# Layer 0 of a four-layer network: blocks of the first and last image overlap, and the table is cleared in 163 small transfers

## The chip, the cores and the metric

The kernel runs on one core of one Trainium2 chip. A core has five engines that work side by side, each on its own list of instructions[...]: TensorE (PE) for matrix products, VectorE (DVE), ScalarE (ACT), GpSimd (POOL), and SyncE (SP), which here only issues transfers between the chip's memory (DRAM) and the on-chip buffer (SBUF). Sixteen DMA engines carry those transfers. PE writes its results to PSUM, a small memory of eight banks. An instruction that needs another engine's result waits on a semaphore, and everything behind it on its own engine waits too.

The metric is the device time of one execution in microseconds (us). Before the change it is 12985.0 us, the median of three runs from 12982.07 to 13003.0.

## The reference

Four images of 128 channels and 48 x 48 pixels go through four layers. The change touches layer 0 and the hand-over to layer 1. Layer 0, cut to what matters (`L` = 2304 pixels, `DI` = 256 inner channels, `K` = 4 scan directions, `N` = 16 states):

```python
def _L0_conv_ref(x, ...):
    def step(h, inp):
        u_t, d_t, B_t, C_t = inp
        dA = jnp.exp(d_t[..., None] * A)
        h = h * dA + (d_t * u_t)[..., None] * B_t[:, :, None, :]
        y = jnp.einsum('bkdn,bkn->bkd', h, C_t)
        return (h, y)
    ...
    xn = _layernorm(xi, ln1_g, ln1_b)
    xz = xn @ in_proj_w.T
    xc, z = jnp.split(xz, 2, axis=-1)
    xc = conv3x3_per_channel(xc) + conv_b          # cut
    xc = jax.nn.silu(xc)
    xs = jnp.stack([x_hw, x_wh, x_hw[..., ::-1], x_wh[..., ::-1]], axis=1)
    ...                                            # delta, B and C from xs
    out_y = _selective_scan(xs, delta, A, Bs, Cs, Ds)
    ...                                            # the four directions are added up to y
    y = _layernorm(y, outn_g, outn_b)
    y = y * jax.nn.silu(z)
    out = xi + y @ out_proj_w.T
```

Layer 1 is a deformable 3 x 3 convolution. Its first step is an ordinary 3 x 3 convolution of layer 0's output to 27 channels (18 offsets and 9 masks for each pixel); the pixels that the offsets point to are then gathered, with zeros outside the image:

```python
off_out = lax.conv_general_dilated(x, w_off, ..., padding='SAME') + b_off
o1, o2, mask = jnp.split(off_out, 3, axis=1)
...
sampled = _bilinear_gather(x, py, px) * mask[:, None]
```

Layers 2 and 3 are attention and mixture-of-experts layers on the same pixels; the change does not touch them.

## The kernel before

Layer 0 (`_layer0`) treats the four images one after another. For each image there are three kinds of work.

**Before the scans** (`pre`, written for one image). An image is cut into six blocks of 384 pixels. `before(im, j)` is a list of ten steps for one block: fetch `x` (L242), turn it on PE so that pixels lie on partitions (L247), copy it out of PSUM on ACT (L251), statistics on DVE with a power on POOL (L207 to L210), standardise on DVE (L214), turn back (L257), scale on ACT and store the result `xn` to DRAM for later (L261, L262), project to the two halves of the inner channels (L266), and copy each half into a padded image (L269). `merged(lists, lag)` joins the lists of the six blocks: list `i` starts `i * lag` steps late, and steps of the same time stand next to each other. With `lag` 10 the blocks simply follow one another. Then come 24 pieces of the per-channel 3 x 3 convolution (`convolve`: nine taps as 18 recorded matmuls, L187, and a copy with bias on ACT, L294) and `activate` (L302). `chained` joins lists so that the last step of one and the first step of the next share a place.

**The scans.** An image has 12 pieces (4 directions x 3 chunks of 768 pixels), each with 16 steps, one per state. A step is written out by hand in the loop at the end of `_layer0`: `row` loads one row of B to all partitions (L500, from the DRAM tensor `rows` that `prepare` stored at L372), `decay` (L505), `times_b` (L512 to L519), `scan` (L545), `turn` and `back` (L559, L573). Between the steps the loop calls `fill()` three times, which takes the next items from lanes: the preparation of the next piece, and an image lane that holds `post` of the image before and `pre` of the image after.

**After the scans** (`post`). `after(im, j)` has 18 steps for a block: fetch `y`, `xn` and `x` (L624 to L628), turn `y` (L634) and copy it (L641), statistics and standardising, turn back (L648), scale (L653), the gate's product (L663, L674), silu with two table loads on ACT (L677, L678), gating (L681), the output product (L686), the residual (L691), a copy into the padded image (L692), turn and store to `tok` (L697 to L702). When the last block is stored, four copies put `tok` into layer 1's `table` (L709). Then `offsets(im, j)`, nine steps for a block: 2 x 9 taps of the 27-channel convolution (L187), copy (L747), turn (L754), copy and store to `offs` (L760, L762).

For images 1 to 3 `pre`, and for images 0 to 2 `post`, lie in the lanes among the scans. `pre` of image 0 (the head) and `post` of image 3 (the tail) stand alone: `for s in pre(images[0]) + prepare(pieces[0], None)` ahead of the loop and `for s in post(images[-1])` behind it.

**PSUM and buffers.** The eight banks are shared out by pools: `ps` has two for the scans' turns, `pf` one, `pu` one for `prepare`, `yp` three and `b0` one. All steps of `before`, `convolve`, `after` and `offsets` take their PSUM from `psum()`, that is from the one bank of `pf`. SBUF buffers come from the pool `sp`, with two buffers for a name unless `bufs` says otherwise.

**The table.** Layer 1 gathers from `table`, which has a border of zeros around each image. It is cleared at the start (L169 to L173): the accumulator `y` is set to zero and written out ten times.

**Order.** The whole of layer 0 is under `manual_schedule` for PE, ACT, DVE and POOL, which keep the written order. SP is not among them: where a transfer stands in SP's list is decided by the planner of the framework, from its own idea of when things are ready.

Of the kernel before, what the change touches and what calls it, by code (L numbers as in the profile page):

```python
# [15 lines left out]
F32 = mybir.dt.float32  # L16
# [7 lines left out]
P = 128  # L24
# [15 lines left out]
CH = 768  # L40
# [59 lines left out]
]  # L100
NPI = len(PIECES)
TPC = CH // P
CT = 512
HBUF = 3
HB = BLK // 2
# [2 lines left out]
def _layer0(ctx, env, dr, io, table, offs):  # L108
# [16 lines left out]
    def load(name, shape):  # L125
        t = cp.tile(shape, F32, name=name)
        nc.sync.dma_start(t, io[name])
        return t

    def psum(*shape):  # L130
        return pf.tile(list(shape), F32, name="pf", tag="pf")

    ln_g = load("l0_ln_g", [P, 1])
# [27 lines left out]
    for pad in pads:  # L161
        nc.gpsimd.memset(pad, 0.0)


    u_hw = wp.tile([P, ND, L], F32, name="u_hw")
    u_wh = wp.tile([P, ND, L], F32, name="u_wh")
    y = wp.tile([P, ND, L], F32, name="y")
    zero = y.rearrange("p d f -> p (d f)")
    nc.gpsimd.memset(zero, 0.0)  # L169
    flat = table.rearrange("r c -> (r c)").rearrange("(p f) -> p f", p=P)  # L170
    for i in range(0, flat.shape[1], ND * L):
        w = min(ND * L, flat.shape[1] - i)
        nc.sync.dma_start(flat[:, i : i + w], zero[:, :w])  # L173


# [136 lines left out]

    def merged(lists, lag):

        out = []
        for t in range(max(i * lag + len(a) for i, a in enumerate(lists))):
            for i, a in enumerate(lists):
                if 0 <= t - i * lag < len(a):
                    out.append(a[t - i * lag])
        return out  # L320

    def chained(lists):
# [8 lines left out]
        return out  # L331

    def pre(im):
        items = merged([before(im, j) for j in range(NBLK)], 10)
        return items + chained([convolve(d, r) for r in range(L // HB) for d in range(ND)]) + [activate]

    class Piece:
# [279 lines left out]
    def after(im, j):  # L617

        cols = bass.ts(j, BLK)
        t = {}  # L620

        def fetch():
            t["yb"] = sp.tile([P, ND, BLK], F32, name="yb", bufs=1)
            nc.sync.dma_start(t["yb"], im.y[:, :, cols])  # L624
            t["xn"] = sp.tile([P, BLK], F32, name="xn")
            nc.sync.dma_start(t["xn"], im.xn[:, cols])
            t["xb"] = sp.tile([P, BLK], F32, name="xb")
            nc.sync.dma_start(t["xb"], io["x"][im.b][:, cols])  # L628

        def turn_y(g0, g1):  # L630
            t["pt"] = pt = psum(P, g1 - g0, DI)
            for g in range(g0, g1):
                for d in range(ND):
                    nc.tensor.transpose(  # L634
                        pt[:, g - g0, bass.ts(d, P)], t["yb"][:, d, bass.ts(g, P)], ident
                    )

        def turned(g0, g1):
            if g0 == 0:
                t["yt"] = sp.tile([P, G3, DI], F32, name="yt", bufs=1)  # L640
            nc.scalar.copy(t["yt"][:, g0:g1, :], t.pop("pt"))  # L641
            if g1 == G3:
                t["first"], t["second"] = standardise(t["yt"])

        def back_y(d):
            t["pt"] = pt = psum(P, BLK)
            for g in range(G3):
                nc.tensor.transpose(pt[:, bass.ts(g, P)], t["yt"][:, g, bass.ts(d, P)], ident)  # L648

        def normed(d):  # L650
            if d == 0:
                t["yn"] = sp.tile([P, ND, BLK], F32, name="yn", bufs=1)
            nc.scalar.activation(  # L653
                t["yn"][:, d, :],
                t.pop("pt"),
                AF.Identity,
                bias=ob[:, d : d + 1],
                scale=og[:, d : d + 1],
            )

        def gate(d):
            t["pz"] = psum(P, BLK)
            nc.tensor.matmul(  # L663
                t["pz"],
                ipT[:, DI + d * P : DI + (d + 1) * P],
                t["xn"],
                start=True,
                stop=True,
            )

        def gate_out(d):
            if d == 0:
                t["z"] = sp.tile([P, ND, BLK], F32, name="yt", bufs=1)
# [60 lines left out]

    def offsets(im, j):
        t = {}

        def third(i, n):
            if n == 0:
                t["pp"] = psum(NOFF, HB)  # L740
            taps(t["pp"], woT, pads[0], 2 * j + i, 3 * n, 3 * n + 3)

        def rows(i):
            if i == 0:
                t["fo"] = sp.tile([P, G3, DI], F32, name="yt", bufs=1)
                t["fo"] = t["fo"].rearrange("p g c -> p (g c)")[:NOFF, :BLK]
            nc.scalar.activation(  # L747
                t["fo"][:, bass.ts(i, HB)], t.pop("pp"), AF.Identity, bias=bo
            )

        def turn():
            t["pt"] = pt = psum(P, G3, NOFF)
# [22 lines left out]

    def post(im):
        return merged([after(im, j) for j in range(NBLK)], 18) + chained(
            [offsets(im, j) for j in range(NBLK)]
        )
# [21 lines left out]
                self.done += 1  # L801

    with tc.manual_schedule(engines=ORDERED):
        for s in pre(images[0]) + prepare(pieces[0], None):
            s()
        for g in range(3):
            do(row, g)
# [13 lines left out]
        for g in range(len(pieces) * NS + 2):  # L821
# [2 lines left out]
            if n == 0 and i + 1 < len(pieces):  # L824
                lanes["next"] = Lane(prepare(pieces[i + 1], pieces[i]), 3 * (NS - 3))
            if (p, n) == (0, 5) and b < NB:
                items = post(images[b - 1]) if b else []
                cols = [lambda d=d, j=j: columns(d, j) for j in range(NCH) for d in range(ND)]
                gap = len(items) // len(cols)
                for q, c in enumerate(cols):  # L830
# [33 lines left out]
            do(scan, g, 1)  # L864
        for d in range(ND):
            collect(pieces[-1], d)
        for s in post(images[-1]):
            s()

# [1359 lines left out]
```

## Time and profile before

| What | Value |
|---|---|
| Median of three runs | 12985.0 us (12982.07 to 13003.0) |
| Profiled execution | 12885.25 us |
| Its span, first to last instruction | 12883.3 us |
| Mean granted TensorE clock | 0.935 |
| Busy over the span | PE 87%, DVE 66%, ACT 54%, POOL 34% |
| First scan starts | 229.8 us |
| Last `y` accumulated | 5218.4 us |
| First and last gather of layer 1 | 5423.0 and 6332.9 us |

The profile is that of one execution, and all its times count from the start of its span. A row of the windows gives a stretch, its length, the busy time of each engine with the number of instructions, the mean TensorE clock that was granted (1.00 is full speed), the share of the 16 DMA engines' time in use, and GB/s. A row of the timeline gives start and length of one instruction or a run of equal ones, its line and shapes, and in brackets how long its engine had been idle and what ended that. A DMA row ends with the median time from a transfer's issue to its landing.

### The profile page before, as it was taken

How to read it: one execution, taken by the hardware profiler on the slowest of the kernel's cores; microseconds unless marked ns; L12 is line 12 of the kernel's file. 1: busy time of each engine (PE TensorE's matmuls, PEld its weight loads, DVE VectorE, ACT ScalarE, POOL GpSimd, SP SyncE). 2: the span in 40 equal slices, each digit the busy share in tenths (PEclk: the TensorE clock that was granted, in tenths of full speed). 3: DMA queues.
4: the chain of work that ended last, by engine and by line, in shares of the span. 5: the costliest groups of instructions: out<-in, count | busy, mean ns of one | idle time of the engine just before them, and what ended most of it. 6: DMA issues, size and time to landing. Idle time of an engine off the chain costs nothing. (4 is left out here: it accounts for less than half of the span.)

```text
span 12883.3 us, 192724 instructions
## 1 busy us (share of the span) xinstructions
PE 11151.3 (87%) x71150; PEld 8431.5 (65%) x71150; DVE 8493.7 (66%) x15424; ACT 6929.4 (54%) x13281; POOL 4401.5 (34%) x4727
## 2 busy tenths in 40 slices
PE   6879788878797887689799999999999997899997
PEld 4667666766676666488677787777877774333333
DVE  4998889888988899455555666566665653444442
ACT  3777777777777777311155655555565653123322
POOL 1443333333333344277643333333333331000000
PEclk9999999999999999799899999999999997799995
DMA  2221222122212222266500000000000003000003
GB/s 104 67 71 63 77 79 71 63 77 80 71 63 75 81 67 67 85 189 197 149 1 3 3 4 2 4 3 3 4 2 3 1 1 117 10 6 7 7 8 120
DMA packets 307846, 677.49 MB, mean 53 GB/s; under 512 B 39109, under 2 KB 128985, under 8 KB 304865
## 3 DMA queue, kind: packets, MB, share of 16 engines
q1 hardware_dynamic: 254032, 493.49, 12.2%
q0 software_dynamic: 51840, 169.91, 4.7%
q8 instruction: 571, 9.36, 0.3%
q14 instruction: 363, 2.97, 0.1%
q10 hardware_dynamic: 1040, 1.77, 0.0%
HBM read 602.63 MB, written 71.85 MB: 52 GB/s over the span
## 5 line engine op out<-in xcount | busy, mean ns | idle before, releaser
L565 ACT ACTIVATE hs<-ps,bct 128x256 f32<-128x256 f32 x4608 | 1853.9, 474 | 1182.0 <-PE ps L559 1130.5
L559 PE MATMUL ps<-ident,h 128*128 128x128 f32 x9216 | 1496.1, 294 | 778.8 <-DVE h L545 608.8
L559 PEld LDWEIGHTS ps<-ident,h 128*128 128x128 f32 x9216 | 1083.0, 148 | 1162.5 <-DVE h L545 716.2
L573 PE MATMUL yp<-ident,hs 128*128 128x128 f32 x9216 | 1408.2, 289 | 28.5 <-ACT ys L588 28.5
L505 ACT ACTIVATE dA<-delta,l_Al 128x768 f32<-128x768 f32 x1536 | 1388.3, 936 | 0.3
L512 POOL TENSOR_TENSOR h<-du,rB 128x512 f32<-128x512 f32 x768 | 1077.5, 1403 | 767.5 <-PE ps L559 689.0
L573 PEld LDWEIGHTS yp<-ident,hs 128*128 128x128 f32 x9216 | 1159.9, 151 | 82.7 <-ACT ys L588 57.6
L545 DVE TENSOR_TENSOR_SCAN h<-dA,h 128x256 f32<-128x256 f32 (+1 forms) x1024 | 1083.4, 1058 | 27.2
L545 DVE TENSOR_TENSOR_SCAN h<-dA,carry,h 128x768 f32<-128x768 f32 x512 | 1027.9, 2008 | 10.6 <-ACT dA L505 10.6
L1180 POOL TENSOR_TENSOR T<-T,bias 128x384 f32<-128x384 f32 x384 | 383.8, 999 | 1560.4 <-DVE fn L1108 1520.2
L487 POOL TENSOR_SCALAR_AFFINE_SELECT dB<-bct 128x512 f32<-128x512 f32 x768 | 748.4, 975 | 385.5 <-PE b L519 244.9
L1953 ACT ACTIVATE pT<-scT 128x768 f32<-128x768 f32 (+2 forms) x504 | 377.6, 749 | 894.2 <-PE scT L1945 894.0
L519 PE MATMUL b<-dB,duT 128*128 128x128 f32 x6144 | 830.2, 279 | 0.8 <-ACT duT L445 0.8
L545 DVE TENSOR_TENSOR_SCAN h<-dA,carry,b 128x512 f32<-128x512 f32 x512 | 645.7, 1261 | 267.8 <-PE b L519 250.5
L949 POOL DMA_INDIRECT g<-table,idx x648 | 710.1, 1096 | 263.6 <-issue 146.4
L519 PEld LDWEIGHTS b<-dB,duT 128*128 128x128 f32 x6144 | 770.7, 197 | 2.4 <-POOL h L512 1.2
L962 PE MATMUL pt<-ident,gw 128*128 128x128 f32 x5184 | 661.9, 283 | 103.3 <-DVE gw L956 100.4
L956 DVE TENSOR_TENSOR gw<-g,wq 128x512 f32<-128x512 f32 x648 | 445.9, 694 | 427.9 <-DMA g<-table,idx 377.3
L962 PEld LDWEIGHTS pt<-ident,gw 128*128 128x128 f32 x5184 | 608.0, 193 | 152.1 <-DVE gw L956 119.7
L552 POOL COPY carry<-h 128x2 f32<-128x2 f32 x512 | 97.3, 190 | 1780.4 <-DVE h L545 1715.2
L1901 DVE TENSOR_REDUCE mx<-sc 128x2 f32<-128x1024 f32 (+3 forms) x400 | 428.5, 1071 | 364.8 <-PE sc L1891 359.8
L516 DVE TENSOR_TENSOR h<-du,rB 128x512 f32<-128x512 f32 x768 | 633.3, 825 | 4.2 <-DMA rB<-rows 4.1
(341 smaller groups left out, 23182.1 us busy)
## 6 DMA issues: line engine op xcount, KB each, us to landing
rB<-rows SPq DMA_DIRECT2D x768, 384.0 KB, 3.5
w<-f_w SPq DMA_DIRECT2D x64, 1024.0 KB, 6.4
table<-y SPq DMA_DIRECT2D x9, 2304.0 KB, 17.8
table<-tok SPq DMA_DIRECT2D x16, 1152.0 KB, 10.4
g<-table,idx POOLq DMA_INDIRECT x648, 3.8
xb<-x SPq DMA_DIRECT2D x48, 192.0 KB, 3.1
xn<-xn SPq DMA_DIRECT2D x48, 192.0 KB, 3.5
yd<-y SPq DMA_DIRECT2D x4, 2304.0 KB
```

The lines of the kernel that those rows point to most:

```text
L487: nc.gpsimd.affine_select(out=x.dB[n], in_=x.bc[:, m0 : m0 + CT // P, n : n + 1].to_broadcast([P, CT // P, P]), pattern=[[0, CT // P], [1, ...
L505: nc.scalar.activation(dA, x.delta[:, d, :], AF.Exp, scale=A[:, d, x.k, n : n + 1])
L512: nc.gpsimd.tensor_mul(h[:, 1, own], x.du[:, 1, own], x.rB[n][:, own])
L516: nc.vector.tensor_mul(x.h[n][:, :, own], x.du[:, :, own], b)
L519: nc.tensor.matmul(b0[:, bass.ts(m, P)], x.duT[:, m, :], x.dB[n][:, m, :], start=True, stop=True,)
L545: nc.vector.tensor_tensor_scan(h, da, b, initial=first, op0=ALU.mult, op1=ALU.add)
L559: nc.tensor.transpose(tt[:, m, bass.ts(d, P)], x.h[n][:, d, bass.ts(2 * q + m, P)], ident)
L565: nc.scalar.activation(hs, tt[:, m, :], AF.Copy, scale=x.bc[:, 2 * q + m, NS + n : NS + n + 1])
L573: nc.tensor.matmul(yp[:, q, (2 * d + m) * P : (2 * d + m + 1) * P], hs[:, bass.ts(d, P)], ident, is_transpose=True, start=n == 0 and m == ...
L949: nc.gpsimd.indirect_dma_start(out=g, out_offset=None, in_=table, in_offset=bass.IndirectOffsetOnAxis(ap=idx[:, j : j + 1], axis=0),)
L956: nc.vector.tensor_mul(gw, g.rearrange("p (q c) -> p q c", c=C), wq[:, i, t, :].unsqueeze(2).to_broadcast([P, 4, C]),)
L962: nc.tensor.matmul(pt[:, t - t0, :], gw[:, q, :], ident, start=q == 0, stop=q == 3)
```

## The change

The change has five parts.

1. A list `banks` is added. While it is empty, `psum()` works as before. While it is filled, with one entry for `pf` and two for `ps`, `psum()` takes the three banks in turn. It is filled for `pre(images[0])`, emptied again, and filled for `post(images[-1])`.
2. With `banks` filled, `pre` starts a block every 3 steps instead of every 10.
3. With `banks` filled, `post` starts an `after` list every 6 steps (before: every 18) and an `offsets` list every 9 steps from step 23 on, merged with them (before: behind them). `merged` takes a list of starts for this.
4. With `banks` filled, the steps of `post` take other buffers: `yb` is a buffer `h` of the scans (three of them), `xn` is `dA0`, `xb` is `rB` (three), `yn` is `dA1`, `z` takes the name `yb`, `fo` is `xd`, and `offsets` takes its PSUM from `pu`.
5. The table is cleared from a tile `zero` of 256 columns in 163 transfers of 128 KB at most. They are written as items of the image lane of image 0, which held only the `columns` copies before.

The diff, cut to its core:

```diff
+ZW = 256
...
+    banks = []
+
     def psum(*shape):
+        if banks:
+            banks.append(banks.pop(0))
+            pool, name = banks[-1]
+            return pool.tile(list(shape), F32, name=name, tag=name)
         return pf.tile(list(shape), F32, name="pf", tag="pf")
...
-    zero = y.rearrange("p d f -> p (d f)")
+
+    zero = cp.tile([P, ZW], F32, name="zero")
     nc.gpsimd.memset(zero, 0.0)
     flat = table.rearrange("r c -> (r c)").rearrange("(p f) -> p f", p=P)
-    for i in range(0, flat.shape[1], ND * L):
-        w = min(ND * L, flat.shape[1] - i)
+
+    def clear(i):
+        w = min(ZW, flat.shape[1] - i)
         nc.sync.dma_start(flat[:, i : i + w], zero[:, :w])
...
     def pre(im):
-        items = merged([before(im, j) for j in range(NBLK)], 10)
+        items = merged([before(im, j) for j in range(NBLK)], 3 if banks else 10)
...
         def fetch():
-            t["yb"] = sp.tile([P, ND, BLK], F32, name="yb", bufs=1)
+            if banks:
+                t["yb"] = sp.tile([P, ND, CH], F32, name="h", bufs=HBUF)[:, :, :BLK]
+                t["xn"] = sp.tile([P, CH], F32, name="dA0")[:, :BLK]
+                t["xb"] = sp.tile([P, CH], F32, name="rB", bufs=3)[:, :BLK]
+            else:
+                ...
...
+        def own(*shape):
+            return pu.tile(list(shape), F32, name="pu", tag="pu") if banks else psum(*shape)
...
     def post(im):
+        if banks:
+            lists = [f(im, j) for f in (after, offsets) for j in range(NBLK)]
+            starts = [6 * j for j in range(NBLK)]
+            starts += [9 * j + 23 for j in range(NBLK)]
+            return merged(lists, starts)
         return merged([after(im, j) for j in range(NBLK)], 18) + chained(
             [offsets(im, j) for j in range(NBLK)]
         )
...
-        for s in pre(images[0]) + prepare(pieces[0], None):
+        free = [(pf, "pf"), (ps, "ps"), (ps, "ps")]
+        banks += free
+        for s in pre(images[0]):
+            s()
+        del banks[:]
+        for s in prepare(pieces[0], None):
             s()
...
             if (p, n) == (0, 5) and b < NB:
-                items = post(images[b - 1]) if b else []
+                if b:
+                    items = post(images[b - 1])
+                else:
+                    items = [lambda i=i: clear(i) for i in range(0, flat.shape[1], ZW)]
...
+        banks += free
         for s in post(images[-1]):
             s()
```

More of the change, by code (lines that the diff above doesn't have):

```diff
@@ L313, in merged @@
     def merged(lists, lag):
+        starts = lag if isinstance(lag, list) else [i * lag for i in range(len(lists))]
         out = []
[L316 to L319, printed above, removed]
+        for t in range(max(i + len(a) for i, a in zip(starts, lists))):
+            for i, a in zip(starts, lists):
+                if 0 <= t - i < len(a):
+                    out.append(a[t - i])
         return out
@@ L622, in fetch @@
         def fetch():
-            t["yb"] = sp.tile([P, ND, BLK], F32, name="yb", bufs=1)
+            if banks:
[3 more added lines that the diff above has]
+            else:
+                t["yb"] = sp.tile([P, ND, BLK], F32, name="yb", bufs=1)
+                t["xn"] = sp.tile([P, BLK], F32, name="xn")
+                t["xb"] = sp.tile([P, BLK], F32, name="xb")
             nc.sync.dma_start(t["yb"], im.y[:, :, cols])
-            t["xn"] = sp.tile([P, BLK], F32, name="xn")
             nc.sync.dma_start(t["xn"], im.xn[:, cols])
-            t["xb"] = sp.tile([P, BLK], F32, name="xb")
             nc.sync.dma_start(t["xb"], io["x"][im.b][:, cols])
@@ L651, in normed @@
             if d == 0:
-                t["yn"] = sp.tile([P, ND, BLK], F32, name="yn", bufs=1)
+                if banks:
+                    t["yn"] = sp.tile([P, CH], F32, name="dA1")
+                    t["yn"] = t["yn"].rearrange("p (d f) -> p d f", d=ND)
+                else:
+                    t["yn"] = sp.tile([P, ND, BLK], F32, name="yn", bufs=1)
             nc.scalar.activation(
@@ L672, in gate_out @@
             if d == 0:
-                t["z"] = sp.tile([P, ND, BLK], F32, name="yt", bufs=1)
+                t["z"] = sp.tile([P, ND, BLK], F32, name="yb" if banks else "yt", bufs=1)
             nc.scalar.copy(t["z"][:, d, :], t.pop("pz"))
@@ L736, in offsets @@
         t = {}
+        def own(*shape):
+            return pu.tile(list(shape), F32, name="pu", tag="pu") if banks else psum(*shape)
         def third(i, n):
             if n == 0:
-                t["pp"] = psum(NOFF, HB)
+                t["pp"] = own(NOFF, HB)
             taps(t["pp"], woT, pads[0], 2 * j + i, 3 * n, 3 * n + 3)
@@ L744, in rows @@
             if i == 0:
-                t["fo"] = sp.tile([P, G3, DI], F32, name="yt", bufs=1)
-                t["fo"] = t["fo"].rearrange("p g c -> p (g c)")[:NOFF, :BLK]
+                if banks:
+                    t["fo"] = sp.tile([NR + 2 * NS, CH], F32, name="xd", bufs=1)
+                else:
+                    t["fo"] = sp.tile([P, G3, DI], F32, name="yt", bufs=1)
+                    t["fo"] = t["fo"].rearrange("p g c -> p (g c)")
+                t["fo"] = t["fo"][:NOFF, :BLK]
             nc.scalar.activation(
@@ L751, in turn @@
         def turn():
-            t["pt"] = pt = psum(P, G3, NOFF)
+            t["pt"] = pt = own(P, G3, NOFF)
             for g in range(G3):
@@ L776, in post @@
     def post(im):
+        if banks:
+            lists = [f(im, j) for f in (after, offsets) for j in range(NBLK)]
+            starts = [6 * j for j in range(NBLK)]
+            starts += [9 * j + 23 for j in range(NBLK)]
+            return merged(lists, starts)
         return merged([after(im, j) for j in range(NBLK)], 18) + chained(
@@ L826, in _layer0 @@
             if (p, n) == (0, 5) and b < NB:
-                items = post(images[b - 1]) if b else []
+                if b:
+                    items = post(images[b - 1])
+                else:
+                    items = [lambda i=i: clear(i) for i in range(0, flat.shape[1], ZW)]
                 cols = [lambda d=d, j=j: columns(d, j) for j in range(NCH) for d in range(ND)]
```

## The prediction

> **What bounds it now.** The page's chain of waits starts beyond 10,000 us and never reaches layer 0, so I read layer 0 in order of time. It splits into a head (0 to 229.8 us, the first scan), the scans (to 5215.5) and a tail up to the first gather of layer 1 (5423). The windows give busy time by engine (PE, PEld, DVE, ACT, POOL), then TensorE clock, DMA share, GB/s:
>
> ```profile
> 10.40:102.50 92.10, 30.61 (x60) 12.29 (x60) 22.60 (x85) 6.89 (x12) 5.12 (x6) 1.00 0.63 257
> 102.50:193.60 91.10, 78.76 (x432) 71.71 (x432) 0.00 (x0) 10.08 (x24) 0.00 (x0) 1.00 0.00 1
> 5226.00:5358.00 132.00, 65.08 (x139) 27.95 (x140) 27.80 (x72) 42.85 (x60) 8.13 (x12) 0.51 0.14 37
> 5358.00:5407.00 49.00, 40.41 (x234) 23.51 (x233) 1.46 (x6) 4.93 (x12) 0.00 (x0) 0.98 0.37 105
> ```
>
> Rows 1 and 3: no engine is busy half the time, so one block's latency is the time, not any engine's work. Row 2 is the 3x3 convolution, row 4 the offset convolution: PE over 80% busy, the rest is waiting for the one PSUM bank `pf`, which every step before, between and behind the scans shares. The scans keep DVE 89% busy (4420.2 of 4985.7) and no line of theirs changes.
>
> The timeline shows why (start, duration, instruction, idle before it and its releaser):
>
> ```profile
> 37.31 0.91 PE L257 MATMUL pf<-ident,xt 128*128 128x128 f32 x3 [3.62 <-DVE xt L214]
> ...
> 64.70 0.67 ACT L261 ACTIVATE xn<-pf,l_ln_b,l_ln_g 128x384 f32<-128x384 f32 x1 [30.46 <-DMA xn<-xn]
> ...
> 102.55 5.33 PE L187 MATMUL pf<-pad,diag 128*128 128x192 f32 x18 [0.65 <-DVE pad L269]
> ...
> 108.48 3.16 PE L187 MATMUL pf<-pad,diag 128*128 128x192 f32 x18 [0.60 <-ACT u_hw L294]
> ```
>
> The second line is a stall: block 2's `xn` buffer is still being stored, and that store queued behind the clearing. From 38.2 to 65.4 PE stands still, 27.2 us. The DMA rows for 15 to 66 us, at 98.9% of 16 engines, say so:
>
> ```profile
> table<-y SPq DMA_DIRECT2D x5, 2304.0 KB, 43.8
> xn<-xn SPq DMA_DIRECT2D x3, 192.0 KB, 34.1
> ```
>
> The other blocks come every 10.83 us (turns at 80.87 and 91.71).
>
> **Head, clearing.** The name says "among the scans", but only PE, ACT, DVE and POOL keep the written order; the planner places what SP issues. In the changed program as built, SP's list holds all 163 clears (128 KB each) ahead of the first `rows` store: one after `xb(1)`, 28 more among the fetches and stores of the six blocks, then 134 in a row behind the last `xn` store. Each waits for the eighth transfer before it. So the scans get nothing extra, and the question is whether 134 clears end before SP is needed for `rows`, which stands behind them.
>
> Cost of one: SP's issue of a 128-partition transfer takes 0.32 to 0.43 us (L500, L127). The old clears moved 430 GB/s in 18 KB runs (131 KB: 0.30 us), the `table<-tok` copies about 295 GB/s in 512 B runs (0.44 us); a clear has 1 KB runs. Eight in flight, landing like an `xn` store when queues are empty (1.8 to 2.0 us), allow one per 0.25 us. I take 0.42: 134 x 0.42 = 56 us. They can start after the last `normed`, about 43, and end near 99; `rows` is wanted at about 134 (below). Spare: (134 - 43)/134 = 0.68 us per clear.
>
> A rule speaks against this. The Trainium skill ("DMA: Bandwidth & Descriptors", section Bandwidth, and its fit under "Anatomy of one DMA") wants transfers of 1 MiB or more and prices one DMA at about 2.0 us plus bytes/436e3, there for GpSimd-issued ones: 2.3 us per clear. Paid one after another that is 308 us, `rows` 217 us late, and the change loses. The rows say that the fixed part overlaps: 384 KB `rB` loads land in 3.5 us yet issue in 0.32. I follow the rows; the rule is the losing rival below.
>
> **Head, blocks.** `lag` 3 instead of 10, three banks instead of one. Durations of before, at the slow clock (128x384 matmuls of 0.83 us; the clock column's 1.00 is no evidence here, since the same kind takes 0.83 where it shows 0.50): PE 0.90 + 0.91 + 2 x 1.65 = 5.1 us per block; ACT 0.48 + 0.67; DVE statistics 1.5, standardise 0.88, two copies 1.12. In three steps, one block's share, the longest loop is copy 0.56, statistics 1.5, POOL's power with its hand-overs 1.2, standardise 0.88, copy 0.56: 4.7. So a block every 5.2 us: 10.4 + 5 x 5.2 + 10.8 = 47 at the slow clock; at full clock 4.7 and 7 us for the last block's latency: 41. I take 46, against 102.55. The 27.2 us stall goes too (it is inside the 102.55): with at most eight transfers in flight, a store finds at most eight clears, 2.4 to 3.5 us, ahead of it instead of 21 MB, and an `xn` buffer has two block periods, 10 us, before its reuse. SP's list waits for `normed` ahead of `xb(4)` and `xb(5)`, but each is issued some 10 us before its turn.
>
> **Head, convolution.** 24 groups of 18 matmuls: 3.19 us each, now 3.71 apart, because the next group waits for ACT's 0.42 us copy and two hand-overs. With three banks the copy lies under the next group: 24 x 3.19 = 76.6, +0.45 for the last copy. 46 + 77 = 123, against 193.6. **Head: -70.5** (slow first group, +2.2: -68; full clock: -76). The 36 us from there to the first scan stay; `rows` is issued 11 us into them (204.5 before, 134 after). The `y` memset (3.9 us, POOL) becomes a short one; both lie under the load of `xb`, which lands at 10.4. The `columns` copies move by at most one place among the scans, and at 1.5 us each on POOL that is nothing.
>
> **Tail, blocks.** Now: six times 21.5 us from 5228.9, then six offset blocks of 8.0, end 5406.4: 177.5. After: blocks start every 6 steps, offsets from step 23 on. Per block PE has 1.12 + 0.69 + 1.18 + 0.90 + 2 x 1.65 + 2.93 + 0.90 = 11.0 us (6.5 at full clock, by the ratio 3.16 to 5.33); ACT 7.1, of it 3.4 for silu with two table loads; DVE 4.8. An offset block has 36 taps (6.2) and a turn (0.4), already at full clock: 6.6.
>
> Here the clock decides. Window row 3 stands at 0.51. The Trainium skill ("TensorE: Matmul & The Clock Gate", Part 1) says that the clock rises after about 3.4 us of sustained work and falls after an idle window. By the row the PE sum is 6 x 11.0 + 39.6 = 106, and walking the built lists of the engines (each instruction starts when its engine, its inputs and its bank or buffer are free) with its durations gives an end 135 after the first turn; the same walk of the lists of before gives 138.8 for its first part, which took 129, so it is a little long. By the rule 6 x 6.5 + 39.6 = 79, and the walk gives 97. At the slow clock PE would be busy 106 of 135, denser than the 72% that layer 1 has at 0.88 (5400 to 5500), and `taps`, now among the blocks, sits at 0.98. So mostly full, slow in the fill: block starts at 0, 7.5, 15, 24, 35, 47, last `out` at 79, then 3.4 offset blocks' worth with their one `pu` bank as before, 28: **107**. **Tail: -70.5** (-42 to -80).
>
> What could be late: `yb`, `xn` and `xb` now take scan buffers (`h`, `dA0`, `rB`) and can't be fetched before the scans end. Three `x` and two `xn` loads, 1 MB, are issued before `yd<-y` at 5218.4 and lie under the last three `ys` copies; 5228.9 stays. The `table` copies take 21 us from the last `out` (5357.8 to the end of the DMA burst near 5379); now 28 us of offsets and 17 of layer 1's set-up cover them. `z` moves to `yb`, `fo` to `xd`, `yn` to `dA1`: free, except that `yt` is one buffer, so ACT's copy waits for `back_y(1)` of the block before, included in the walk.
>
> **Sum.** -70.5 - 70.5 = -141. The profiled execution would go from 12885.3 (span 12883.3, 2 us around it) to 12744. It lies 100 us below the median 12985.0; I subtract from the median: **12844**.
>
> **Rivals.** *(1) Mostly half clock in the tail, slow first groups:* -68 - 42 = 12875. For: 0.51 today, with the fill unchanged. Against: density. *(2) Both at full clock:* -76 - 80 = 12829. *(3) Clears late but not fatal:* beyond 0.68 us per clear each 0.1 us costs 13.4; at 1.0 us, 43: 12887. *(4) Slower:* the same place, `rows` behind 134 clears on SP. From (134 + 141 - 43)/134 = 1.73 us per clear the whole gain is gone; at the skill's 2.3, +76: 13061. Against: eight in flight would have to land in 14 us each. *(5) Layer 1 waits instead:* its first gather needs the last `offs` store and the `table` copies; if copies and stores on SP delay it by all the tail gains, only the head is left: 12914.
>
> **Chances.** Likeliest (12830 to 12862) 0.60; (1) 0.18; (2) 0.07; (3) and (5) 0.08; nothing within 0.2% (26 us, about what three runs can tell) 0.03; slower 0.04. So faster 0.93, same 0.03, slower 0.04. Range: both clock ends with the runs' spread, 12818 to 12888.
>
> **What would show it.** Right: first scan near 159; first convolution group near 46 and groups 3.2 apart; no 30 us wait on `xn`; `table<-zero` over by about 100; first gather near 5282 (5423 - 141); clock above 0.8 in the tail. Wrong: `rows` issued late after the clears; tail clock at 0.5; PE in the tail waiting for `yb` or for ACT's table loads.

## The result, and the profile after

The changed kernel takes **12823.4 us** (median of four, 12783.6 to 12849.1) against 12985.8 before (four, 12982.1 to 13003.0): ratio 0.987, interval 0.985 to 0.989, 162 us less. I had predicted 12844. The direction and both places of the gain are right; both gains were put too small. The interval allows 139 to 200 us, so the time alone can't tell the predicted 141 from the measured 162; the stages can.

The table cuts layer 0 and its neighbours at the same instructions in three profiles. The third column is the kernel before, profiled once more (the first experiment below), and it is the one to compare with: the profile that the prediction was read from had an unusually short gather in layer 1.

| stage, us | before, first profile | before, again | after | after minus again |
|---|---|---|---|---|
| head: start to first scan | 229.8 | 229.2 | 145.1 | -84.1 |
| scans: to the issue of the last `yd<-y` | 4988.6 | 4981.0 | 4975.9 | -5.2 |
| tail: to the first gather of layer 1 | 204.6 | 205.3 | 126.8 | -78.5 |
| layer 1: first to last gather | 909.9 | 1002.2 | 1004.8 | +2.6 |
| the rest | 6550.4 | 6565.6 | 6529.3 | -36.2 |
| span | 12883.3 | 12983.3 | 12781.9 | -201.4 |

The head and the tail make -162.6, as does the difference of the medians (-162.4); that the two agree so closely is luck, given the interval. The scans and the rest vary by such amounts with no cause in the code: over the other profiles of these kernels in which SP follows its planner, the scans took 4977 to 4991 us and the rest 6548 to 6588. The changed kernel's profiled execution, the fastest of its four, was low in both.

Windows of the kernel after (bounds, us, busy time of PE, PEld, DVE, ACT and POOL, then TensorE clock, DMA share, GB/s): head blocks, convolution, tail up to the last `out`, tail to the last offset copy.

```profile
10.20:39.80 29.60, 19.42 (x61) 10.87 (x62) 18.66 (x74) 6.89 (x12) 5.12 (x6) 1.00 0.59 194
39.80:110.60 70.80, 70.39 (x433) 70.09 (x431) 0.67 (x2) 10.04 (x24) 0.00 (x0) 1.00 0.75 248
5131.90:5204.40 72.50, 58.70 (x247) 32.92 (x248) 27.36 (x74) 42.97 (x64) 8.14 (x12) 0.83 0.20 56
5204.40:5229.90 25.50, 20.81 (x123) 12.07 (x123) 0.73 (x3) 3.36 (x8) 0.00 (x0) 1.00 0.69 198
```

The same work as in the four windows of before: 92 us have become 29.6, 91 have become 70.8, 132 have become 72.5, 49 have become 25.5. In the convolution PE now has hardly a gap, while the DMA engines carry the clears at 248 GB/s beside it. The tail's block part has a mean clock of 0.83, where it had 0.51. The mean is made of stretches at the half and at the full clock, as two windows inside the tail show:

```profile
5131.90:5142.40 10.50, 6.75 (x22) 4.71 (x22) 4.69 (x17) 3.51 (x7) 0.86 (x1) 0.50 0.31 86
5152.80:5159.50 6.70, 3.72 (x16) 1.98 (x16) 2.23 (x4) 6.05 (x8) 0.85 (x1) 1.00 0.46 137
```

The timeline of ACT, PE and DVE in the head after (start, duration, instruction, idle before it and its releaser):

```profile
20.52 0.67 ACT L270 ACTIVATE xn<-pf,l_ln_b,l_ln_g 128x384 f32<-128x384 f32 x1 [1.40 <-PE pf L266]
25.54 0.67 ACT L270 ACTIVATE xn<-ps,l_ln_b,l_ln_g 128x384 f32<-128x384 f32 x1 [1.45 <-PE ps L266]
29.88 0.67 ACT L270 ACTIVATE xn<-ps,l_ln_b,l_ln_g 128x384 f32<-128x384 f32 x1 [1.82 <-PE ps L266]
...
23.32 1.49 PE L275 MATMUL pf<-xn,l_ipT 128*128 128x384 f32 x2
...
31.68 0.81 PE L275 MATMUL ps<-xn,l_ipT 128*128 128x384 f32 x2
...
39.80 3.09 PE L196 MATMUL pf<-pad,diag 128*128 128x192 f32 x18
42.72 3.58 PE L196 MATMUL ps<-pad,diag 128*128 128x192 f32 x21
...
19.88 0.56 DVE L278 COPY pad<-ps 128x384 f32<-128x384 f32 x1 [1.17 <-PE ps L275]
...
28.64 1.02 DVE L278 COPY pad<-ps 128x384 f32<-128x384 f32 x2
```

The wait of 30 us for `xn` is gone. The same pair of 128x384 records takes 1.49 us at 23 and 0.81 at 31: the clock rose in between. (The clock column says 1.00 for the whole window, but the trace's first record of the clock is the rise itself, at 25.9, so for the time before it the column is no evidence.) With it the step from block to block went from 5.0 us to 4.3, and DVE's wait of 1.17 us for the second projection went away. The first convolution group has a record of 3.09 us, yet the next starts 2.92 later: I read this as the drain of the last result, which the next group overlaps. SP, in the same kernel (SPq is what SP issues):

```profile
38.38 0.32 SPq L271 DMA_DIRECT2D xn<-xn  x1
38.74 70.77 SPq L182 DMA_DIRECT2D table<-zero  x134
109.63 0.86 SPq L251 DMA_DIRECT2D xb<-x  x2
121.52 0.33 SPq L383 DMA_DIRECT2D rows<-xd  x1
```

The 134 clears in a row take 0.528 us each and are over 12 us before SP issues `rows`, at 121.5.

### The profile page after: what moved, and what is told of

Its sections match the earlier page's. It is cut to its first block, busy times and chain, and to the rows that moved or that the text cites. A ratio compares the mean times of both kernels' runs of the same rounds, so it can differ in the third digit from the quotient of the medians.

```text
span 12781.9 us, 192881 instructions
## 1 busy us (share of the span) xinstructions
PE 11081.7 (87%) x71150; PEld 8430.2 (66%) x71150; DVE 8468.7 (66%) x15424; ACT 6928.7 (54%) x13281; POOL 4339.4 (34%) x4727
## 5 line engine op out<-in xcount | busy, mean ns | idle before, releaser
L556 DVE TENSOR_TENSOR_SCAN h<-dA,h 128x256 f32<-128x256 f32 (+1 forms) x1024 | 1082.8, 1057 | 27.2
L990 POOL DMA_INDIRECT g<-table,idx x648 | 657.9, 1015 | 389.3 <-DVE gw L997 178.1
L1003 PEld LDWEIGHTS pt<-ident,gw 128*128 128x128 f32 x5184 | 640.5, 204 | 202.9 <-DVE gw L997 141.9
```

Source lines behind the costliest of these rows:

```text
L556: nc.vector.tensor_tensor_scan(h, da, b, initial=first, op0=ALU.mult, op1=ALU.add)
L990: nc.gpsimd.indirect_dma_start(out=g, out_offset=None, in_=table, in_offset=bass.IndirectOffsetOnAxis(ap=idx[:, j : j + 1], axis=0),)
L1003: nc.tensor.matmul(pt[:, t - t0, :], gw[:, q, :], ident, start=q == 0, stop=q == 3)
```

## Experiments

### The kernel before, once more

The change is nil.

> The kernel before, unchanged, profiled once more. Theory A (the length of layer 1's gather varies from execution to execution): its profile has either 910 us from the first to the last gather of layer 1, as before, or about 1005, as in the changed kernel, and its own time follows (12885 or about 12980); the timed runs lie near 12985. Theory B (the length belongs to the build): 910 within 10 us again, span within 10 us of 12883, and the timed runs' 100 us more come from somewhere else. Ratio 1.000 by both.

Measured 12996.0 us (ratio 1.001, interval 1.000 to 1.002), span of the profile 12983.3, layer 1's gather 1002.2. So the 100 us that lay between the profiled execution and the median lie in layer 1's gather. Theory A is nearer, but the later runs show that the length goes with the chip rather than with the execution: the ten profiles taken on two chips, whatever the kernel, have a gather of 1000 to 1008 us; the two taken on a third have 901 and 905, and there the kernel before took 12886.7 at the median. (The chip of the first profile is not on record; its 12885.25 is like the third chip's. Chip and hour changed together, so that it is the chip itself is not shown.) The gather's windows, first in the first profile of before, then in the second, in the columns as above:

```profile
5423.00:6333.00 910.00, 823.60 (x6564) 766.78 (x6565) 464.50 (x735) 122.35 (x286) 712.54 (x649) 0.99 0.68 192
```

```profile
5415.50:6417.70 1002.20, 851.70 (x6538) 806.06 (x6539) 445.89 (x733) 121.42 (x285) 658.98 (x648) 0.93 0.61 174
```

The same work takes 92 us longer at a clock of 0.93 and 174 GB/s. This says that both kernels must be compared on the same chip, and that the difference of layer 1 between the first profile and the one after is none of the change's doing.

### One part at a time

The head's overlap alone leaves out the tail's `banks += free` and brings the old clearing back; the clearing alone leaves out both lines `banks += free`; the tail alone leaves out the first of them and brings the old clearing back:

```
-    zero = cp.tile([P, ZW], F32, name="zero")
+    zero = y.rearrange("p d f -> p (d f)")
...
-    def clear(i):
-        w = min(ZW, flat.shape[1] - i)
+    for i in range(0, flat.shape[1], ND * L):
+        w = min(ND * L, flat.shape[1] - i)
...
-                    items = [lambda i=i: clear(i) for i in range(0, flat.shape[1], ZW)]
+                    items = []
```

> Only the head's blocks and convolution overlap (three banks, 3 steps apart); the table is cleared at the start in large transfers and the tail is as before. My theory: block 2 still waits for the store of xn behind the clearing until about 64.7 us, where the changed kernel has it at 25.5; all later steps of the head are 39 us later than in the changed kernel, so the convolution starts near 79 and the first scan near 184 (before 229.8, changed 145.0): -46. Rival (the gain is the overlap alone and the clearing is beside the point): first scan within 5 us of 145. Layer 1's gather 910 or 1005 by theory A; by theory B one of the two in every run of this build.

> Only the clearing is changed (163 transfers of 128 KB); one bank, 10 steps apart, and the tail as before. My theory: the 27.2 us wait of block 2 goes and nothing else in the head changes, so blocks every 10.8 us, groups of the convolution 3.71 apart, first scan at 229.8 - 27 = 203 (the diag build is 2 us earlier besides: 201). With head only at -46 this makes -73, 12 less than the -84.8 of both together, because the wait hides 12 us less of the blocks when they are fast. Rival (the wait was only swapped for one behind small clears): first scan after 215.

> Only the tail is changed (three banks, blocks 6 steps apart, offsets among them). My theory: from the first turn to the last offset copy 98 us instead of 177, first gather of layer 1 some 80 us earlier counted from the first scan, head as before (first scan near 230). Time: -79 against the kernel before, if the layer 1 gather is in the same mode. Theory B (the build sets the gather's length): this build, which has the tail's code and so layer 1's new start, shows about 1005 and the gain is given back: 0 to +16.

| | first scan | tail, to first gather | gather | time | interval of the ratio |
|---|---|---|---|---|---|
| head only | 189.1 | 207.1 | 1002.8 | 12951.5 | 0.996 to 0.998 |
| clearing only | 201.6 | 206.4 | 1007.8 | 12951.9 | 0.997 to 0.998 |
| tail only | 229.5 | 127.2 | 1003.9 | 12898.7 | 0.992 to 0.996 |

(Before on the same chip: 12988.8.) Theory B falls: all three have the long gather, as before does there. The two parts of the head make -40 and -28 alone and -84 together, 16 us more than their sum. The timeline of ACT with the head's overlap and the old clearing shows most of these 16:

```profile
21.69 0.67 ACT L270 ACTIVATE xn<-pf,l_ln_b,l_ln_g 128x384 f32<-128x384 f32 x1 [1.34 <-PE pf L266]
23.73 0.48 ACT L260 COPY xt<-ps 128x384 f32<-128x384 f32 x1 [1.37 <-PE ps L256]
65.42 0.67 ACT L270 ACTIVATE xn<-ps,l_ln_b,l_ln_g 128x384 f32<-128x384 f32 x1 [41.21 <-DMA xn<-xn]
```

The store of `xn` lands at 65 with either order of the blocks, because it stands behind the clearing; a faster block only waits longer for it, 41 us here against 30 before. With fast blocks the old clearing holds up this third `xn` by 39.9 us (65.42 against 25.54 in the changed kernel), with slow ones by 27.7 (64.71 in the kernel before, 37.05 with the new clearing alone): 12 of the 16. The other 4, which make the head-only run 5 us later than expected, come behind the stall: 2 in the remaining blocks, more than half of whose time was at the half clock again, and 2 between the convolution and the first scan, for which I have no cause. The new clearing thus pays twice: once by its own wait, once by letting the overlap count. The tail gains its 78 us without either.

### The convolution's banks

```
-                t["pp"] = psum(P, HB)
+                t["pp"] = pf.tile([P, HB], F32, name="pf", tag="pf")
```

> The changed kernel with the head's convolution on one PSUM bank, as before; the blocks keep three. My theory: groups 3.71 apart again instead of 2.92, 24 x 0.79 = 19 us, first scan at 164 instead of 145. Rival (the groups are nearer together because of something else, such as the clock): less than 5 us.

Measured: first scan 165.4, where 164 was expected, and 12840.1 us. The timeline of PE in this kernel:

```profile
40.70 3.09 PE L196 MATMUL pf<-pad,diag 128*128 128x192 f32 x18
44.40 3.17 PE L196 MATMUL pf<-pad,diag 128*128 128x192 f32 x18 [0.60 <-ACT u_hw L303]
48.07 3.19 PE L196 MATMUL pf<-pad,diag 128*128 128x192 f32 x18 [0.51 <-ACT u_hw L303]
```

The groups are 3.70 apart again, and the records are 3.1 to 3.2 long as with three banks. Of the 20.4 us on the first scan, 18.0 lie in the convolution itself (88.8 us against 70.8), 0.9 ahead of it and 1.5 behind it. The figure that the sum needed was the distance of back-to-back groups, 2.93, not the length of a record. The clears beside the convolution cost it nothing: with the head's overlap and the old clearing, whose transfers are over by then, it takes the same 70.7 us with idle DMA engines:

```profile
81.80:152.50 70.70, 70.70 (x433) 70.61 (x431) 0.56 (x1) 9.67 (x23) 0.00 (x0) 0.99 0.00 1
```

### The clock

Matmuls that nobody reads were put ahead of the head's first block and between its first steps; then into the tail of the kernel *before*, to raise the clock there without any overlap:

```
+    def warm(n):
+        p = pu.tile([P, P], F32, name="pu", tag="pu")
+        for i in range(n):
+            nc.tensor.matmul(p, ident, ident, start=i == 0, stop=i == n - 1)
...
+        warm(30)
+        for q, s in enumerate(pre(images[0])):
...
+            if q < 10:
+                warm(6)
```

> The changed kernel with idle matmuls on the identity ahead of layer 0's first block (30 of them, while PE waits for the first xb) and 6 more behind each of the first ten steps; their result is read by nobody. My theory (the clock sets part of the head: in the changed kernel the 128x384 matmuls take 0.8 us until 26 us and 0.45 after): full clock from the first block, blocks 4.2 us apart from the start instead of 5.0, first convolution group at 36 instead of 39.8, first scan near 141. Rival (the blocks' pace is the DVE and ACT steps and the clock is beside the point, the added matmuls only stand in the way): convolution at 40 to 42, first scan 145 to 147. The rest as in the changed kernel.

> The kernel before, with 30 idle matmuls ahead of the tail's first block and 8 behind each step of its block part. It separates the clock from the overlap in the tail's 79 us. My theory: the granted clock goes from 0.51 to above 0.9 in the block part, a block takes 17.5 us instead of 21.5 (my walk of the queues gives 112.5 to 138.8 for six, full to half clock), and the tail from its first turn to the last offset copy takes about 153 instead of 177: -24 on the span. So of the 79 us the clock alone is 24 and the overlap 55. Rival (the block is a chain through ACT, DVE and the hand-overs and the added matmuls lengthen it): 177 or more, no gain.

Both missed their purpose: one such product takes 0.25 us at the full clock (eight in 1.95 us), more than I had counted, so that the added work stood in the way. In the head (12838.9 us) the first turn came at 13.6 instead of 10.2 and the convolution at 49.9, neither what the theory nor what the rival said, and the clock's share in the head stays open. In the tail (13091.6 us, 102 more than before) PE was busy 133 of 135 us:

```profile
5225.00:5360.00 135.00, 133.02 (x1062) 122.87 (x1061) 16.06 (x42) 23.62 (x34) 4.93 (x7) 1.00 0.10 26
```

The clock did go to 1.00, and the block's own matmuls took the 5.5 us that the next expectation starts from. The same tail again, with fewer of them:

```
+        few = [2, 0, 1, 0, 4, 4, 3, 2, 1, 1, 2, 1, 4, 4, 3, 2, 1, 2]
+        for q, s in enumerate(post(images[-1])):
+            warm(10 if q == 0 else few[q % 18] if q < 18 * NBLK else 0)
```

> The kernel before with fewer idle matmuls in the tail than the run that saturated PE with them: 10 ahead of the first block, and 37 per block, most of them where the block waits for statistics, for silu and for the added x, so that they take 9 us of a block at 0.25 us each (measured at full clock) and stand little in its way. In the saturated run the block's own matmuls took 5.5 us per block at the full clock, in the kernel before 11.0 at the half clock. My theory (the clock alone is worth what PE's share of the chain shrinks by): at full clock six blocks take up to 33 us less, less 6 us of idle matmuls in the way: first turn to last offset copy 150 instead of 177, -27. So of the tail's 79 us about 30 are clock and the rest overlap. Rival (the clock falls back to half, or the chain is bound elsewhere): 172 or more.

Its windows over the six blocks and over the offsets:

```profile
5217.00:5326.90 109.90, 100.98 (x579) 76.90 (x580) 27.42 (x72) 42.85 (x60) 8.14 (x12) 0.96 0.16 42
5326.90:5374.00 47.10, 39.09 (x231) 22.93 (x232) 1.22 (x5) 4.93 (x12) 0.00 (x0) 1.00 0.38 110
```

At a clock of 0.96 with one bank the blocks take 109.9 us, against 129.0 in the kernel before, and the whole tail from its first turn (5217.0) to the last offset copy (5374.0) takes 157.0, against 177.0: **-20**, with the added matmuls partly in its way. The time, 12966.6 against 12980.1 (interval 0.9985 to 1.0002), agrees but could not have shown it. The rival's 172 is out, and the 150 of my theory was not reached. So the clock alone, without any overlap, is worth at least 20 of the tail's 79 us, and the other 59 at most need the overlap. No run has the overlap at the half clock, so how the two add up is not shown. One edit gave both: with the blocks overlapped PE was busy 81% of the block part instead of 49%, and the mean clock rose from 0.51 to 0.83.

### What the clears cost, and where they stand

```
-ZW = 256
+ZW = 128
```

> The changed kernel with 326 clears of 64 KB (512 B in a row) in place of 163 of 128 KB. It puts the slower rival to the test: rows stands behind all clears on SP. My theory: a transfer has a price of its own, about 0.45 us on SP (the issue of a 128 KB clear took 0.447 us at the median), so some 267 clears behind the last xn store end at 40 + 120 = 160, rows goes out there instead of at 121.5, and the first scan starts 39 us later, at 184. Rival (the price is the bytes': 0.26 us each): the clears end near 110 as before and the first scan stays at 145.

Measured: first scan 146.2, 12821.7 us. SP in this kernel, by its timeline:

```profile
39.53 82.67 SPq L182 DMA_DIRECT2D table<-zero  x164
122.31 0.37 SPq L383 DMA_DIRECT2D rows<-xd  x1
122.72 1.85 SPq L182 DMA_DIRECT2D table<-zero  x4
124.67 1.32 SPq L511 DMA_DIRECT2D rB<-rows  x3
126.03 13.68 SPq L182 DMA_DIRECT2D table<-zero  x26
```

The price is per transfer, as I had it: 82.67/164 = 0.504 us for 64 KB, against 0.528 us for 128 KB in the changed kernel. Most of it is SP's own issue, 0.43 us at the median for 64 KB and 0.45 for 128 KB. A price by the bytes (0.26) is out, although the first scan stayed where that rival had put it: SP's planner did not leave `rows` behind twice as many clears; it set it after 164 of them and sent the others later. So the delay that rival (4) of the prediction speaks of was not tried. It was tried by writing the clears between the blocks and the first piece:

```
+        for i in range(0, flat.shape[1], ZW):
+            clear(i)
         for s in prepare(pieces[0], None):
```

> The 326 clears of 64 KB again, now issued in the written order between the blocks and the first piece, so that 297 of them stand in a row on SP ahead of the first store of rows (the run before showed only about 164 ahead of it: there SP's planner had put rows between them). This is my rival (4) made to happen. At 0.504 us each, as that run measured, the row of clears ends at 39.5 + 297 x 0.504 = 189 and rows goes out then, not at 121.5. In the changed kernel 22 us lie between the store of rows and the first use of rB, of which I count about 5 for the store and one load, so some 15 us of cover: first scan at 189 - 121.5 - 15 = 52 later, 197 (212 if there is no cover), and the time as much above the changed kernel's. Rival (SP or the DMA engines catch up, or rows is not on the path): first scan within 5 us of 145.

```profile
38.98 144.85 SPq L182 DMA_DIRECT2D table<-zero  x297
183.93 0.37 SPq L383 DMA_DIRECT2D rows<-xd  x1
```

At 0.488 us each, `rows` goes out at 183.9, 62.4 us later than in the changed kernel, and the first scan starts at 191.1, 46.0 later (52 expected). The mechanism of rival (4) is real, with 16.4 us of cover between `rows` and its user that the prediction did not count. The time was 12769.4 where before took 12886.7 on that chip: -117, which is the 162 less the 46. In the changed kernel 134 clears have from 38.7 to 121.5, or 0.62 us each, 0.74 with that cover. Last, the clears really among the scans:

```
-    with tc.manual_schedule(engines=ORDERED):
+    with tc.manual_schedule(engines=ORDERED | {mybir.EngineType.SP}):
```

> The changed kernel with SP also bound to the written order in layer 0, so that the 163 clears really go out among the scans (two or three between two rB loads, the first behind the ninth rB load) and none lies in the head. My theory: in the changed kernel the clears are wholly hidden in the head, so it gains nothing there: convolution at 38 to 40, first scan at 143 to 146; the scans, with the clears beside them, stay at 4976 to 4991. Time within 0.2% of the changed kernel's. Rival (the clears slow the head's loads and stores): first scan 5 us or more earlier. Other rival (the clears or the written order delay rB loads in the scans): scans 10 us or more longer.

```profile
16.43 0.33 SPq L271 DMA_DIRECT2D xn<-xn  x1
16.86 0.37 SPq L251 DMA_DIRECT2D xb<-x  x1
22.92 0.33 SPq L271 DMA_DIRECT2D xn<-xn  x1
23.35 0.37 SPq L251 DMA_DIRECT2D xb<-x  x1
```

12765.0 against the same 12886.7: 122 us faster than before, where the changed kernel, not run on that chip, should be 162 faster. My theory missed on all its figures. The written order puts each `xb` load behind the store of an `xn` that isn't ready (the planner issues the first such load at 11.1, here it goes at 16.9), so blocks come 6.5 us apart, the convolution starts at 49.7 and the first scan at 157.7. The scans take 5005.5, 15 to 30 us more than in the others, as the second rival had it. That rival named two causes, and the trace tells them apart. Below are the clears (shortest, median and longest issue in ns, then first and last start), and DVE's products with `rB` from 157 to 1500 us and from 1500 to 5170 (busy, mean ns, then idle time and what ended it):

```profile
L182 SPq DMA_DIRECT2D table<-zero x163: 320/431/983, 180.6 to 616.0; - x163
L527 DVE TENSOR_TENSOR h<-du,rB 128x512 f32<-128x512 f32 x215 | 181.1, 843 | 0.0
L527 DVE TENSOR_TENSOR h<-du,rB 128x512 f32<-128x512 f32 x553 | 457.8, 828 | 16.2 <-DMA rB<-rows 16.2
```

While the clears go out, DVE never waits for `rB`, and the scans keep pace: the 231st scan instruction, at 605.6, starts 447.9 us after the first, and 448.1 after it in the changed kernel. The waits, 16.2 us against at most 4.6 in every other profile, come long after the last clear. So it is the written order of SP's transfers that delays the scans, not the clears beside them. What the head would be without clears stays open, since its blocks are held up by `xb` here. The run does show that the place where the planner put the clears, against the change's wording, is better than among the scans with this order.

### Layer 1's buffers

```
-                    g = sp.tile([P, 4 * C], F32, name="g", bufs=8)
+                    g = sp.tile([P, 4 * C], F32, name="g", bufs=12)
-                    gw = sp.tile([P, 4, C], F32, name="gw", bufs=4)
+                    gw = sp.tile([P, 4, C], F32, name="gw", bufs=8)
```

> The changed kernel with more buffers in layer 1's gather: 12 instead of 8 for g, 8 instead of 4 for gw. In eight profiles of these kernels the gather from first to last start took 1000 to 1008 us, with the granted clock falling to 0.5 for 3.4 to 6.8 us some 30 times; in one, the first of the kernel before, 910 with two falls. Theory D (a fall of the clock fills gw and g, POOL stops gathering, PE then starves and the clock falls again; deeper buffers break the circle): below 940 us and fewer than ten falls, -65 to -95 on the time. Rival (the falls come from PE's own pauses, whatever the buffers): 990 or more and about 30 falls, no change.

Theory D falls: gather 1003.7 us, 26 falls of the clock (21 in the changed kernel), 12831.8 us. The groups of layer 1's first matmul, weight loads, in the changed kernel and in this one (busy, mean ns, then idle time and what ended it):

```profile
L1003 PEld LDWEIGHTS pt<-ident,gw 128*128 128x128 f32 x5118 | 633.2, 204 | 202.9 <-DVE gw L997 141.9 <-issue 52.3
```

```profile
L1003 PEld LDWEIGHTS pt<-ident,gw 128*128 128x128 f32 x5111 | 639.4, 204 | 164.2 <-issue 148.4 <-DVE gw L997 7.1
```

With more buffers PE hardly waits for `gw` any more (7.1 us for 141.9), but pauses for nothing that the profile shows (148.4 for 52.3), and the stage is as long as before. Of the rival, about 30 falls and 990 us or more came true; its cause, that the falls come from PE's own pauses, is not shown. What makes PE pause there, and why not on the third chip, stays open.

## Where the prediction was right, and which terms of its sum failed

**Place and sign.** Head and tail, and nothing else, carry the gain; the reading of `lag`, banks and the stall holds, each part shown alone. The first gather came at 5247.8 where I expected 5282; 13 of these 34 us are shorter scans (4975.9 against 4988.6), which no line of the change accounts for.

**What failed.** Three terms of the sum, all put too long, some 21 us together: the head's blocks and the tail's blocks, which I costed between the half and the full clock, and the head's convolution, where I took a record's length for a period. Measured were 39.8 for 46, 98.0 for 107, and 70.8 for 77.

**Head, blocks: 46 predicted, 39.8 measured.** I counted 10.4 + 5 x 5.2 + 10.8 and leaned to the end of my bounds that has the half clock (47); the measured time lies even below the other end, 41. From the first block's turn (10.2) to the last block's (31.35) are 21.2 us, where I counted 26; from there to the convolution 8.4, where I counted 10.8. The step was 5.0 at the half clock and 4.3 and less at the full one, which set in at 26 us. The clock's share in that is not shown: in the run with idle matmuls, two steps at the full clock were 4.0 and 4.9 us.

**Head, convolution: 77 predicted, 70.8 measured** (39.8 to 110.6). 24 x 3.19 counted a record's length as a period; 24 x 2.93 + 0.45 = 70.8. The view of before could have said so: with one bank the distance of 3.71 is a record of 3.19 and 0.51 of waiting, so there the drain is on the path. With three banks it isn't. That is the other 6 us of the head; the stretch behind the convolution was 34.5 instead of 36.

**Head, the stall and the clears.** Right: 27.2 us by the clearing alone (27.6 measured), and no block waits for `xn` after. A clear was taken at 0.42 us and cost 0.53; the spare of 0.68 was 0.62, from an earlier `rows`. The price of one transfer, paid in full by each, was rightly set aside: 134 of them took 71 us, not 308. Yet the mechanism that I gave 4 in 100 needs only more clears on the wrong side of `rows`, as the run with 297 of them showed.

**Tail: 107 predicted, 98.0 measured** (5131.9 to 5229.9). The term is the clock of the fill, the first part of the tail, in which the six blocks get under way. The skill's rule and the row of before stood against each other, giving 97 and 135; I took a value between, for a slow fill. The clock was indeed low for 24 of the block part's 72.5 us (that is its mean of 0.83), 21 of them in the first 31. Yet the blocks started at 0, 7.0, 13.4, 23.8, 34.3 and 44.2 where I had 47 for the last, and the last turn of `out` came at 72.5 (full-clock walk 71.9, my value 79). Then 25.5 us of offsets followed instead of 28, at the old pace of 8.0 a block. That the slow fill costs next to nothing, since its blocks wait for statistics and ACT anyway, is argued from this agreement, not shown by a run of its own. The Trainium skill's rule ("TensorE: Matmul & The Clock Gate", Part 1), that sustained work raises the clock, was the better guide than the row of before, and the kernel before with idle matmuls shows that the same blocks do run at 0.96 when PE is kept busy.

**The sum.** -141 should have been -162: 14 more in the head, 8 more in the tail. Rival (2), both at the full clock, has 12829 and lies nearest, but in part by luck: it has the same mistake in the convolution (6 us), and it supposes a full clock from the start, which neither the head (half until 26 us) nor the tail had. I had given it 0.07, and leaned to the slow end twice. Rivals (1), (3) and (5) did not occur. To subtract from the median rather than from the profiled execution was right: that execution came with a gather that the timed runs did not have.

## What to carry to other kernels

Before a latency-bound stage is given more overlap, cost its matmuls at the clock that the denser stage will have, not at the one its sparse form shows; a slow row is partly the effect of the waits that are being removed. Take the distance of back-to-back instructions for a stage that will be back to back, and a record's length only where something waits for its end. And when small transfers are spread by a planner, read where they stand in the queue: it is their number ahead of the first transfer that is waited for, times a price per transfer, that decided here, and between 64 and 128 KB hardly their size.

## What the runs showed of the hardware

- A store of 64 KB (512 B in a row) cost 0.488 to 0.504 us of SP's time and one of 128 KB (1 KB in a row) 0.53, in rows of well over a hundred: half the bytes bought almost nothing.
- The granted clock is 0.5 or 1.0 in all fourteen traces, in stretches that are multiples of 3.41 us; values between are means. It followed how busy PE was: 0.51 in the tail's blocks of before (PE busy 49%), 0.83 with the blocks overlapped (81%), 0.96 with idle matmuls between them (92%).
- The kernel before took 12988.8 and 12886.7 us on two chips, and the profiles taken there differ in one stage by as much (gather of layer 1: 1002 to 1008 against 901 to 905 us). That is 0.8%, which many changes are not worth.
